# Two graph layers on one core: layer 1's weights turned through DRAM and VectorE, block results grown in place, v's bias joined to the output's, a new order of steps

## The chip, the cores and the metric

The kernel runs on one core of a Trainium2 chip. The metric is device time in microseconds of a whole launch, all loads and stores included. All data is float32.

## What is computed

128 batches of 128 nodes with 512 features pass through two layers, both with the same 128 x 128 adjacency. Layer 0 is attention with 8 heads; layer 1 weighs a node's neighbours by a leaky sum of two scores and puts an elu behind.

```python
def layer0(x):                       # Wq, Wk, Wv, Wo: 512 x 512
    q, k, v = x @ Wq + bq, x @ Wk + bk, x @ Wv + bv      # in 8 heads of 64
    s = q @ k.T / 8 + (1 - adj) * -1e9
    return (softmax(s) @ v) @ Wo + bo
def layer1(x):                       # W: 512 x 512, a = (a1, a2)
    h = x @ W
    e = leaky_relu((h @ a1)[:, :, None] + (h @ a2)[:, None, :], 0.2) * adj
    return elu(softmax(e) @ h + beta * h)
x = layernorm(x + layer0(x))
x = layernorm(x + layer1(x))
```

Layer 1 is computed in another order than written: the weights plus beta on the diagonal, A = softmax(e) + beta I, are applied to x first, and (A x) W is then one product.

## The kernel before, in words

Two batches make a group; there are 64 groups (`NG`). For each group five products with 512 x 512 weights are needed: q, k, v, the output product w and layer 1's h. Each is done by a scheme of seven half-size products in place of eight: the weights and the two batches are cut in 2 x 2 blocks, sums of blocks are made ahead (`weight_sum` once, `block_sum` on GpSimd per group), and the products 1, 2, 6, 7, 5, 3, 4 (`product`, lines 267 to 299) are added to each other into the four blocks of the result. Tiles named p (pq, pk, pv, pw, ph) and e (eq, ev, ew, eh) are their banks in PSUM. A q or k product is four matmuls of 128 columns, a v, w or h product two of 256; in the trace each fp32 matmul is two records.

Results leave PSUM in two ways. `take_part` (products 1, 6, 5) copies a product to a part buffer in SBUF, on ScalarE (for w on VectorE, which adds the residual). `take_block` (product 3) puts one straight into its block, and `add_block` (products 2, 7, 4) adds a product to a part and writes the block, on VectorE.

The other steps of a group, in the order of the data:

- `fetch_blocks`, `turn_x`: x is loaded in blocks and turned on VectorE (32 x 32 blocks, so the load does the outer part of the turn).
- `scores` (psc, line 381): 16 matmuls in a group, each on 64 of the 128 rows of the array. `mask`, `row_max`, `exps`, `row_inv`, `normalise` make the softmax on VectorE and ScalarE.
- `attn_write`, `attn_read`, `turn_attn`: the attention weights go to DRAM and come back with their 32 x 32 blocks in place, and VectorE turns the blocks.
- `attend` (po, line 456): 16 matmuls, each on 64 of the 128 columns. `attend_evict` (line 466) copies po to oT on VectorE and adds v's bias, which holds for each row because the softmax's rows sum to one.
- product w, with x + bo (`residual`, on GpSimd) added as it leaves; `bn_stats` and `norm_c` for the layer norm; `row_product` for layer 1's two scores.
- `spread_s2` (pb, line 535): two transposes on TensorE that spread the second score over all rows. `edge`, `leaky`, `edge_max`, `edge_exp`, `edge_inv`, `weights` make A in the tile att.
- `turn_weights` (pat, line 578): two transposes of A on TensorE; `weights_evict` (line 581) copies them to attT on ScalarE.
- `aggregate` (pz, line 591), `aggregate_evict`, product h, then elu, the second layer norm and `store`.

Nothing is scheduled at run time. `rows(g)` and `last_rows(g)` list each step with a place in us, relative to the group's start at g x `STEP` (line 19). For some groups, the first and the last, `other` gives a different list of places. `lay` collects them all, and the pieces are emitted sorted by place under `manual_schedule`: this sorted list is the order of the instructions on each engine, and each engine does its own in that order. The places come from a planner's costs and due times, and are not times of the chip. Groups overlap: a group's steps span about 170 us of places, so that while one is in its q and k products, the one before is in its w product and the one before that in its h product. All products draw on eight PSUM banks (`ps_mm`). DMAs of x, blocks, attention weights and stores are all issued from SP's queue, in the order of the list.

```python
    for g in range(NG):
        lay(g)
    ...
    with tc.manual_schedule():
        for _, _, fn, args in sorted(pieces, key=lambda p: p[:2]):
            fn(*args)
```

Of the kernel before, what the change touches and what calls it, by code (L numbers as in the profile page):

```python
# [13 lines left out]
P = 128  # L14
# [4 lines left out]
STEP = 37.33  # L19
# [3 lines left out]
def gnn_two_layers(  # L23
# [197 lines left out]
    xT, right, tx, qT, kT, vb, y, hp, main, side, part, oT, zT, xr = ({} for _ in range(14))  # L221
# [79 lines left out]
    def take(name, g, n, dst, half):  # L301

        src = region(name, g, n)
        if name in "vh":
            nc.scalar.copy(dst, src)  # L305
        else:
            for m in range(2):
                col = BIAS[name][:, 2 * half + m : 2 * half + m + 1]
                nc.scalar.activation(  # L309
                    dst[:, m, :], src[:, m * N : (m + 1) * N], AF.Identity, bias=col  # L310
                )

    def take_part(name, g, n, i, j):

        shape = [P, 2, N] if name in "qk" else [P, HF]
        t = wk2.tile(shape, F32, tag=f"part{name}{n}", name=f"part_{name}{n}_{g}", bufs=1)
        if name == "w":
            res = xr[g * G + j][:, i * HF : (i + 1) * HF]
            nc.vector.tensor_tensor(t, region(name, g, n), res, ALU.add)  # L319
        else:  # L320
            take(name, g, n, t, i)
        part[name, g, n] = t

# [31 lines left out]
    def take_block(name, g, i, j):  # L355
        dst = block(name, g, i, j)
        if name == "w":
            res = xr[g * G + j][:, i * HF : (i + 1) * HF]
            nc.vector.tensor_tensor(dst, region(name, g, 3), res, ALU.add)
        else:  # L360
            take(name, g, 3, dst, i)

    def add_block(name, g, i, j, n, m):
        src = region(name, g, n)
        if name in "qk":
            src = src.rearrange("p (m n) -> p m n", m=2)
        nc.vector.tensor_tensor(block(name, g, i, j), src, part.pop((name, g, m)), ALU.add)
# [95 lines left out]
    def attend_evict(b):  # L463

        oT[b] = wk2.tile([P, NC, N], F32, tag="oT", name=f"oT_{b}")
        nc.vector.tensor_tensor(  # L466
            oT[b], po.pop(b),
            later["bv"].rearrange("p (m o) -> p m o", o=1).broadcast_to([P, NC, N]), ALU.add,
        )
# [66 lines left out]

    def pair_rows(d, g, tag):
        if g not in d:
            d[g] = wk2.tile([P, G, N], F32, tag=tag, name=f"{tag}_{g}", bufs=1)
        return d[g]  # L540
# [27 lines left out]
    def weights(g, i):  # L568
        nc.vector.scalar_tensor_tensor(
            pair_rows(att, g, "att")[:, i, :], ee[g][:, i, :], einv[g][:, i : i + 1], beta_i,  # L570
            ALU.mult, ALU.add,
        )
# [66 lines left out]
    def at(place, fn, *args):  # L639
        pieces.append((place, len(pieces), fn, args))  # L640

    def rows(g):
# [3 lines left out]
            (-34.63, fetch_blocks, g), (-26.63, turn_x, g, 0), (-25.97, turn_x, g, 1),  # L646
            (-22.82, block_sum, "x", g, 1), (-22.08, block_sum, "x", g, 2),
            (-20.60, block_sum, "x", g, 3), (-19.86, block_sum, "x", g, 4),
            (-18.00, product, "q", g, 1), (-15.88, take_part, "q", g, 1, 0, 0),
            (-13.62, product, "k", g, 1), (-12.73, product, "q", g, 2),  # L650
            (-12.51, take_part, "k", g, 1, 0, 0), (-11.83, product, "k", g, 2),
            (-10.94, product, "q", g, 6), (-10.04, product, "k", g, 6),
            (-9.82, take_part, "q", g, 6, 1, 0), (-9.42, add_block, "k", g, 0, 0, 2, 1),
            (-9.15, product, "q", g, 7), (-8.93, take_part, "k", g, 6, 1, 0),
            (-8.00, product, "k", g, 7), (-7.11, product, "q", g, 5), (-6.81, fetch_x, b0),
            (-6.21, product, "k", g, 5), (-6.00, take_part, "q", g, 5, 1, 1),
            (-5.61, add_block, "q", g, 0, 0, 2, 1), (-5.53, fetch_x, b1),
            (-5.12, add_block, "q", g, 1, 1, 7, 5), (-5.10, take_part, "k", g, 5, 1, 1),
            (-4.45, product, "q", g, 3), (-4.22, add_block, "k", g, 1, 1, 7, 5),
            (-3.55, product, "k", g, 3), (-3.34, take_block, "q", g, 0, 1),  # L660
            (-2.44, take_block, "k", g, 0, 1), (-1.79, product, "q", g, 4),
            (-0.89, product, "k", g, 4), (0.10, add_block, "q", g, 1, 0, 4, 6),
            (0.19, residual, b0), (0.52, add_block, "k", g, 1, 0, 4, 6), (1.47, residual, b1),
            (1.97, scores, b0), (3.09, scores, b1), (3.31, mask, b0, 0), (3.98, mask, b0, 1),
            (4.44, product, "v", g, 1), (4.65, row_max, b0), (5.31, product, "v", g, 2),
            (5.53, take_part, "v", g, 1, 0, 0), (5.87, mask, b1, 0), (6.09, exps, b0, 0),
            (6.54, mask, b1, 1), (7.21, row_max, b1), (7.91, exps, b0, 1), (8.70, exps, b0, 2),
            (9.49, exps, b0, 3), (9.53, add_block, "v", g, 0, 0, 2, 1), (10.50, row_inv, b0),
            (10.92, normalise, b0, 0), (11.50, product, "v", g, 6), (11.52, normalise, b0, 1),
            (12.37, product, "v", g, 7), (12.59, take_part, "v", g, 6, 1, 0),  # L670
            (12.97, normalise, b0, 2), (13.57, normalise, b0, 3), (14.17, exps, b1, 0),
            (14.39, attn_write, b0), (14.96, exps, b1, 1), (16.45, exps, b1, 2),
            (16.72, product, "v", g, 5), (17.24, exps, b1, 3), (17.39, attn_read, b0),
            (18.03, take_part, "v", g, 5, 1, 1), (18.25, row_inv, b1), (18.67, normalise, b1, 0),
            (19.27, normalise, b1, 1), (19.52, add_block, "v", g, 1, 1, 7, 5),
            (20.25, normalise, b1, 2), (20.85, normalise, b1, 3), (21.67, attn_write, b1),
            (24.67, attn_read, b1), (25.56, turn_attn, b0, 0), (28.33, turn_attn, b0, 1),
            (31.06, turn_attn, b1, 0), (32.01, product, "v", g, 3),
            (33.10, take_block, "v", g, 0, 1), (33.53, turn_attn, b1, 1),
            (34.67, product, "v", g, 4), (35.76, add_block, "v", g, 1, 0, 4, 6),  # L680
            (37.33, attend, b0), (38.43, attend, b1), (38.65, attend_evict, b0),
            (45.35, product, "w", g, 1), (45.76, attend_evict, b1), (46.22, product, "w", g, 2),
            (46.44, take_part, "w", g, 1, 0, 0), (46.66, block_sum, "w", g, 3),
            (47.31, add_block, "w", g, 0, 0, 2, 1), (47.40, block_sum, "w", g, 1),
            (48.14, block_sum, "w", g, 2), (50.57, product, "w", g, 6),
            (51.44, product, "w", g, 7), (51.66, take_part, "w", g, 6, 1, 0),
            (53.32, block_sum, "w", g, 4), (54.92, product, "w", g, 5),
            (56.01, take_part, "w", g, 5, 1, 1), (56.43, add_block, "w", g, 1, 1, 7, 5),
            (57.55, product, "w", g, 3), (58.42, product, "w", g, 4),
            (58.64, take_block, "w", g, 0, 1), (59.06, bn_stats, y, b1, "c"),  # L690
            (59.75, bn_aggr, b1, "c"), (59.95, add_block, "w", g, 1, 0, 4, 6),
            (60.37, bn_stats, y, b0, "c"), (61.06, bn_aggr, b0, "c"), (61.26, add_eps, g, "c"),
            (61.43, row_product, b0, 0), (62.16, row_product, b0, 1), (62.89, inv_std, g, "c"),
            (63.61, row_product, b1, 0), (64.34, row_product, b1, 1), (65.07, scale_s, g),
            (66.32, norm_c, b0), (66.41, spread_s2, g), (66.88, edge, g, 0), (67.20, edge, g, 1),
            (67.53, leaky, g), (67.95, edge_max, g), (71.52, norm_c, b1), (72.88, edge_exp, g),
            (74.26, edge_inv, g), (74.43, weights, g, 0), (77.41, weights, g, 1),
            (78.65, turn_weights, g), (79.32, weights_evict, g), (80.84, aggregate, b0),
            (81.76, aggregate, b1), (81.98, aggregate_evict, b0), (84.42, product, "h", g, 1),
            (84.94, aggregate_evict, b1), (85.29, product, "h", g, 2),  # L700
            (86.21, block_sum, "h", g, 1), (86.78, take_part, "h", g, 1, 0, 0),
            (86.95, block_sum, "h", g, 2), (87.38, add_block, "h", g, 0, 0, 2, 1),
            (87.69, block_sum, "h", g, 4), (88.43, block_sum, "h", g, 3),
# [291 lines left out]
```

## Time and profile before

| | |
|---|---|
| time before, median of 3 runs | 2417.62 us (2417.3 to 2419.12) |
| the profiled execution's own time | 2414.03 us |
| its span, first to last instruction | 2412.2 us |
| TensorE busy in the span, matmuls / weight loads | 2387.4 / 2205.3 us |
| VectorE, ScalarE, GpSimd busy | 1957.7, 1485.5, 860.8 us |
| DMA | 245.30 MB, mean 102 GB/s |
| mean granted TensorE clock | 0.998 |

The views use short names: PE is TensorE's matmuls, PEld its weight loads, DVE VectorE, ACT ScalarE, POOL GpSimd, SP the engine whose queue issues most DMAs. Times are us unless marked ns. L289 is line 289 of the kernel. "pq<-xT,wq_sb" reads: writes tile pq from tiles xT and wq_sb; "128*64" is the part of TensorE's array that is used, rows by columns. In a timeline a row is a run of equal instructions with its start, its length and how many they are; matmuls overlap, so the length of a row reaches past the start of the next. In a table of groups, "x128 | 87.7, 686 | 16.5 <-PE po" says: 128 instructions, 87.7 us busy, 686 ns each, 16.5 us of idle time of the engine ahead of them, most of it ended by TensorE's po.

### The profile page before, as it was taken

How to read it: one execution, taken by the hardware profiler on the slowest of the kernel's cores; microseconds unless marked ns; L12 is line 12 of the kernel's file. 1: busy time of each engine (PE TensorE's matmuls, PEld its weight loads, DVE VectorE, ACT ScalarE, POOL GpSimd, SP SyncE). 2: the span in 40 equal slices, each digit the busy share in tenths (PEclk: the TensorE clock that was granted, in tenths of full speed). 3: DMA queues.
4: the chain of work that ended last, by engine and by line, in shares of the span. 5: the costliest groups of instructions: out<-in, count | busy, mean ns of one | idle time of the engine just before them, and what ended most of it. 6: DMA issues, size and time to landing. Idle time of an engine off the chain costs nothing.

```text
span 2412.2 us, 50040 instructions
## 1 busy us (share of the span) xinstructions
PE 2387.4 (99%) x17956; PEld 2205.3 (91%) x17956; DVE 1957.7 (81%) x4385; ACT 1485.5 (62%) x5310; POOL 860.8 (36%) x1045
## 2 busy tenths in 40 slices
PE   8999999999999999999999999999999999999998
PEld 8899999999999999999999999999999999999986
DVE  7788888888888887888888888888888787888887
ACT  4665665666656656666566566665665666656655
POOL 6332332333324323333243233332342333334322
PEclk9999999999999999999999999999999999999999
DMA  5323424334234243343342432433424324234332
GB/s 181 106 91 94 118 77 114 103 82 123 85 101 122 72 115 110 79 120 93 93 123 71 114 107 78 123 90 95 122 76 111 107 78 123 92 93 123 84 109 70
DMA packets 201336, 245.30 MB, mean 102 GB/s; under 512 B 18736, under 2 KB 149808, under 8 KB 200704
## 3 DMA queue, kind: packets, MB, share of 16 engines
q1 hardware_dynamic: 200144, 240.98, 34.7%
q8 instruction: 142, 2.33, 0.4%
q0 software_dynamic: 400, 0.86, 0.1%
q14 instruction: 106, 0.87, 0.1%
q10 hardware_dynamic: 544, 0.26, 0.0%
HBM read 141.37 MB, written 100.66 MB: 100 GB/s over the span
## 4 chain that ended last, share of the span: by engine, by line
PE 92%; DVE 3%; DMA 2%; ACT 1%; SPq 1%; issue 1%; POOL 0%; ACTq 0%; DVEq 0%; POOLq 0%
PE pw L289 11%; PE ph L289 11%; PE pq L295 11%; PE pv L289 11%; PE pk L295 11%; PE eq L295 9%; PE psc L381 5%; PE po L456 5%; PE pz L591 5%; PE ev L289 4%; PE eh L289 4%; PE ew L289 4%; PE pat L578 1%; DMA wv_sb<-in_L_gnn_Wv_dram 1%; ACT sb L417 1%
## 5 line engine op out<-in xcount | busy, mean ns | idle before, releaser
L403 ACT ACTIVATE s<-s,nmax 128x128 f32<-128x128 f32 x1024 | 397.7, 394 | 5.0 <-DVE nmax L397 5.0
L417 ACT ACTIVATE sb<-s,rinv 128x128 f32<-128x128 f32 x1024 | 327.1, 392 | 33.9 <-DVE rinv L410 22.9
L248 POOL TENSOR_TENSOR tw<-oT 128x256 f32<-128x256 f32 x63 | 45.7, 726 | 741.8 <-DVE oT L466 741.8
L437 POOL TENSOR_TENSOR x<-x,bo_b_in 128x512 f32<-128x512 f32 x128 | 164.0, 1291 | 381.0 <-DMA x<-in_x_dram 380.2
L309 ACT ACTIVATE part_q<-pq,bq_c 128x128 f32<-128x128 f32 x384 | 118.7, 360 | 236.9 <-PE pq L295 236.9
L403 ACT ACTIVATION_READ_ACCUMULATOR s<-s,nmax 128x1 f32 x1024 | 196.7, 192 | 0.0
L309 ACT ACTIVATE part_k<-pk,bk_c 128x128 f32<-128x128 f32 x384 | 119.9, 363 | 114.5 <-PE pk L295 67.0
L581 ACT COPY attT<-pat 128x256 f32<-128x256 f32 (+1 forms) x65 | 24.0, 368 | 266.5 <-PE pat L578 266.5
L389 DVE SCALAR_TENSOR_TENSOR s<-psc,amask 128x512 f32<-128x512 f32 x256 | 164.6, 683 | 25.1 <-PE psc L381 25.1
L446 DVE STREAM_TRANSPOSE attnT<-ab 128x512 f32<-128x512 f32 x256 | 178.8, 701 | 4.6 <-DMA ab<-scr 4.1
L506 DVE SCALAR_TENSOR_TENSOR ya<-w,wa_row 128x512 f32<-128x512 f32 x256 | 175.9, 687 | 4.4
L397 DVE TENSOR_REDUCE nmax<-s 128x8 f32<-128x1024 f32 x128 | 156.2, 1220 | 4.4
L319 DVE TENSOR_TENSOR part_w<-pw,x 128x256 f32<-128x256 f32 x189 | 79.4, 420 | 83.5 <-PE pw L289 83.1
L295 PE MATMUL pk<-xT,wk_sb 128*128 128x128 f32 x1024 | 139.9, 280 | 0.0
L228 DVE STREAM_TRANSPOSE xT<-xblk 128x512 f32<-128x512 f32 x128 | 134.7, 1096 | 5.1 <-DMA xblk<-in_x_dram 5.1
L295 PE MATMUL pq<-xT,wq_sb 128*128 128x128 f32 x1024 | 134.9, 275 | 0.8 <-DMA wq_sb<-in_L_gnn_Wq_dram 0.8
L295 PEld LDWEIGHTS pq<-xT,wq_sb 128*128 128x128 f32 x1024 | 129.4, 192 | 4.2 <-issue 1.0
L295 PEld LDWEIGHTS pk<-xT,wk_sb 128*128 128x128 f32 x1024 | 129.3, 192 | 3.9
L381 PE MATMUL psc<-kT,qT 64*128 64x128 f32 x2048 | 132.4, 279 | 0.0
L305 ACT COPY part_v<-pv 128x256 f32<-128x256 f32 x192 | 69.8, 364 | 99.3 <-PE pv L289 99.3
L381 PEld LDWEIGHTS psc<-kT,qT 64*128 64x128 f32 x2048 | 119.5, 188 | 12.1 <-issue 11.8
L591 PEld LDWEIGHTS pz<-attT,x 128*128 128x128 f32 x1024 | 124.3, 192 | 4.1 <-ACT attT L581 0.6
(676 smaller groups left out, 6588.2 us busy)
## 6 DMA issues: line engine op xcount, KB each, us to landing
scr<-sb SPq DMA_DIRECT2D x128, 512.0 KB, 2.7
ab<-scr SPq DMA_DIRECT2D x512, 128.0 KB, 3.1
x<-in_x_dram SPq DMA_DIRECT2D x128, 256.0 KB, 5.0
out_dram<-u SPq DMA_DIRECT2D x128, 256.0 KB, 2.1
xblk<-in_x_dram SPq DMA_DIRECT2D x254, 128.0 KB, 5.5
wq_sb<-in_L_gnn_Wq_dram SPq DMA_DIRECT2D x1, 1024.0 KB, 8.2
wk_sb<-in_L_gnn_Wk_dram SPq DMA_DIRECT2D x1, 1024.0 KB, 10.4
wv_sb<-in_L_gnn_Wv_dram SPq DMA_DIRECT2D x1, 1024.0 KB, 12.7
```

What stands on the lines that cost most here:

```text
L289: nc.tensor.matmul(out, b[:, c, :], a[:, c, :], start=first and c == 0, stop=(c == 1), skip_group_check=True,)
L295: nc.tensor.matmul(out[:, m * N : (m + 1) * N], a[:, c, m * P : (m + 1) * P], b[:, c, :], start=first and m == 0 and c == 0, stop=(c == 1) ...
L309: nc.scalar.activation(dst[:, m, :], src[:, m * N : (m + 1) * N], AF.Identity, bias=col)
L381: nc.tensor.matmul(psc[b][j][:, m, :], qT[g][feats, m, rows], kT[g][feats, m, rows], start=True, stop=True,)
L389: nc.vector.scalar_tensor_tensor(s_t[b][:, j * HP : (j + 1) * HP, :], psc[b][j], SCALE, amask.rearrange("p (o n) -> p o n", o=1).broadcast ...
L397: nc.vector.tensor_reduce(nmax[b], s_t[b], AX.X, ALU.max, negate=True)
L403: nc.scalar.activation(s_t[b][:, h, :], s_t[b][:, h, :], AF.Exp, bias=nmax[b][:, h : h + 1], accum_out=rsum[b][:, h : h + 1],)
L417: nc.scalar.mul(sb[b][:, :, h, :], s_t[b][:, h, :].rearrange("p (b c) -> p b c", c=Q), rinv[b][:, h : h + 1],)
L437: nc.gpsimd.tensor_tensor(xr[b], xr[b], later["bo"], ALU.add)
L446: nc.vector.transpose(attnT[b].rearrange("p h (a r) -> p a h r", r=Q)[:, rows], ab[b].rearrange("p a (h c) -> p a h c", c=Q)[:, rows],)
L506: nc.vector.scalar_tensor_tensor(z, y[b], 1.0, wa_row[j], ALU.mult, ALU.mult, accum_out=s12[g][:, i, j : j + 1])
L591: nc.tensor.matmul(pz[b][:, c, :], x1[b][:, c * P : (c + 1) * P], attT[g][:, i, :], start=True, stop=True,)
```

## The change

- In groups 0 to 61 (`by_blocks`) layer 1's weights are no longer turned on TensorE. `weights` writes att with its 32-column blocks outermost; `weights_write` sends it to DRAM (128 KB, 1 KB a row), four `weights_read` bring it back with blocks in place (32 KB each, runs of 256 bytes), and `weights_turn` turns the 32 x 32 blocks on VectorE into attT. The last two groups keep `turn_weights`.
- `attend_evict` becomes a plain copy on ScalarE. v's bias is carried through the output product once: `bias_product` makes bv @ Wo on TensorE, `bias_add` adds it to bo.
- Part buffers go. `take_part` (now products 1, 6, 5 and 3) writes the block itself, and `add_block` adds a product to the block in place. The engines of these steps stay as they were.
- `STEP` goes from 37.33 to 36.928, and the lists of places are all new: `rows`, `last_rows` (which now has a list for each of the last two groups), `other`, and the places of the weights' loads and sums. In the steady order the two batches' scores have v's and w's first products between them; `attend` comes for the second batch first; w1's load comes after wo's.

```diff
-STEP = 37.33
+STEP = 36.928
...
-    def take_part(name, g, n, i, j):
-
-        shape = [P, 2, N] if name in "qk" else [P, HF]
-        t = wk2.tile(shape, F32, tag=f"part{name}{n}", name=f"part_{name}{n}_{g}", bufs=1)
...
+    def take_part(name, g, n, i, j):
+
+
+        src, dst = region(name, g, n), block(name, g, i, j)
+        if name in "vh":
+            nc.scalar.copy(dst, src)
+        elif name == "w":
             res = xr[g * G + j][:, i * HF : (i + 1) * HF]
-            nc.vector.tensor_tensor(dst, region(name, g, 3), res, ALU.add)
+            nc.vector.tensor_tensor(dst, src, res, ALU.add)
...
-        nc.vector.tensor_tensor(block(name, g, i, j), src, part.pop((name, g, m)), ALU.add)
+        nc.vector.tensor_tensor(dst, src, dst, ALU.add)
...
     def attend_evict(b):
-
         oT[b] = wk2.tile([P, NC, N], F32, tag="oT", name=f"oT_{b}")
-        nc.vector.tensor_tensor(
-            oT[b], po.pop(b),
-            later["bv"].rearrange("p (m o) -> p m o", o=1).broadcast_to([P, NC, N]), ALU.add,
-        )
+        nc.scalar.copy(oT[b], po.pop(b))
+
+
+    bop = {}
+
+    def bias_product():
+        bop[0] = ps_mm.tile([P, D], F32, tag="mm", name="bop")
+        for c in range(NC):
+            nc.tensor.matmul(
+                bop[0], later["bv"][:, c : c + 1].broadcast_to([P, P]), wo_sb[:, c, :],
+                start=(c == 0), stop=(c == NC - 1),
+            )
+
+    def bias_add():
+        nc.vector.tensor_tensor(later["bo"], bop[0], later["bo"], ALU.add)
...
+    def by_blocks(g):
+
+        return g < NG - 2
+
+    def weights_write(g):
+        att_d[g] = scr.tile([P, 4, G * Q], F32, tag="attd", name=f"attd_{g}")
+        nc.sync.dma_start(
+            out=att_d[g].rearrange("p b e -> p (b e)"), in_=att[g].rearrange("p i n -> p (i n)")
+        )
+
+    def weights_read(g):
+        ab2[g] = wk2.tile([P, 4, G * Q], F32, tag="ab2", name=f"ab2_{g}", bufs=1)
+        for n in range(4):
+            nc.sync.dma_start(
+                out=ab2[g][n * Q : (n + 1) * Q],
+                in_=att_d[g][:, n, :].rearrange("(a r) e -> r a e", r=Q),
+            )
+
+    def weights_turn(g):
+        nc.vector.transpose(
+            pair_rows(attT, g, "attT").rearrange("p i (a r) -> p a i r", r=Q),
+            ab2[g].rearrange("p a (i c) -> p a i c", c=Q),
+        )
...
-            (1.97, scores, b0), (3.09, scores, b1), (3.31, mask, b0, 0), (3.98, mask, b0, 1),
-            (4.44, product, "v", g, 1), (4.65, row_max, b0), (5.31, product, "v", g, 2),
...
+            (1.047, scores, b0), (2.042, product, "v", g, 1), (2.317, mask, b0, 0),
+            (2.472, mask, b0, 1), (3.328, scores, b1), (4.811, row_max, b0),
+            (5.124, product, "v", g, 2), (5.419, take_part, "v", g, 1, 0, 0),
...
+            (34.656, add_block, "v", g, 4, 1, 0), (35.86, attend, b1), (36.604, attend, b0),
+            (39.077, attend_evict, b1), (39.294, attend_evict, b0), (39.343, product, "w", g, 1),
...
+            (73.77, weights, g, 1), (75.158, weights_write, g), (75.942, weights_read, g),
+            (81.449, weights_turn, g), (84.036, aggregate, b0), (85.026, aggregate, b1),
...
-        own = last_rows(g) if g == NG - 1 else rows(g)
+        own = rows(g) if g < NG - 2 else last_rows(g)
...
-    at(15.205, load_weight, w1_sb, w1)
-    at(15.265, load_later)
...
-    at(21.105, load_weight, wo_sb, wo)
...
+    at(-2.505, load_later)
...
+    at(13.895, load_weight, wo_sb, wo)
...
+    at(16.595, load_weight, w1_sb, w1)
...
+    at(26.176, bias_product)
...
+    at(29.816, bias_add)
```

## The prediction

> **What bounds the kernel now.** I read the page first, then the chain of waits over some laps, then TensorE's timeline. The page:
>
> ```profile
> span 2412.2 us, 50040 instructions
> PE 2387.4 (99%) x17956; PEld 2205.3 (91%) x17956; DVE 1957.7 (81%) x4385; ACT 1485.5 (62%) x5310; POOL 860.8 (36%) x1045
> PE   8999999999999999999999999999999999999998
> ```
>
> TensorE has work in every slice, and no other engine is near it. The chain of waits, in order of time, repeats itself once per group of two batches:
>
> ```profile
> 714.28 1.90 PE po L456 x32
> 739.40 0.98 PE pk L295 x8
> 751.26 1.90 PE po L456 x32
> ```
>
> One lap is 751.26 - 714.28 = 36.98 us, wholly TensorE. A product that TensorE no longer does is saved, and whatever slows its stream is paid. So I take the stream apart. In TensorE's timeline a step's price is the start of the next row less its own start:
>
> ```profile
> 712.33 1.05 PE L295 MATMUL eq<-tx,wq_sb 128*128 128x128 f32 x8
> 713.22 1.06 PE L295 MATMUL eq<-tx,wk_sb 128*128 128x128 f32 x8
> 714.21 1.97 PE L456 MATMUL po<-attnT,v 128*64 128x128 f32 x32
> 716.11 2.06 PE L381 MATMUL psc<-kT,qT 64*128 64x128 f32 x32
> 718.09 0.44 PE L578 MATMUL pat<-ident,att 128*128 128x128 f32 x2
> 718.37 1.89 PE L289 MATMUL pv<-wv_sb,xT 128*128 128x256 f32 x8
> ```
>
> A q or k product takes 0.89 us, but 0.99 when po follows, which works in half-width tiles (128*64). Both batches' scores (psc, 64*128) together take 1.98, the two transposes of the weights (pat) 0.28, of which only 0.22 is work: the like pair pb takes 0.21 elsewhere (742.90 to 743.11). Near the end the score runs of the two batches stand apart:
>
> ```profile
> 2350.50 1.16 PE L381 MATMUL psc<-kT,qT 64*128 64x128 f32 x16
> 2351.59 1.13 PE L289 MATMUL pw<-wo_sb,oT 128*128 128x256 f32 x4
> 2352.65 1.16 PE L381 MATMUL psc<-kT,qT 64*128 64x128 f32 x16
> 2353.74 1.13 PE L289 MATMUL pv<-wv_sb,xT 128*128 128x256 f32 x4
> 2354.71 1.03 PE L289 MATMUL pw<-s_w,tw 128*128 128x256 f32 x4
> 2355.57 0.60 PE L289 MATMUL pv<-s_v,tx 128*128 128x256 f32 x2
> ```
>
> Each run takes 1.09, the product between them 1.06 and the one after 0.97, where an undisturbed one takes 0.86. Every change of tile shape costs.
>
> **The Trainium skill.** "TensorEngine Tiling (Array Packing)", Key Properties, says that changing the tiling mode, not just the tile, drains TensorE. The trace agrees: about 0.1 us on each side of a change. It gives no figure; I use the trace's. "DMA: Bandwidth & Descriptors", Anatomy of one DMA, puts a fixed cost of about 2 us on a DMA, most of it the receipt; here 256 KB stores land in 2.1 us, 512 KB writes in 2.7, reads in 3.1. Its section on small descriptors charges 27% for 256-byte ones, the size of the new reads; no such transfer is in this trace. "VectorE: DVE Perf Modes", The three transpose paths: VectorE turns 32x32 blocks only, which is why the new path needs the DRAM trip.
>
> **The change, part by part.** Counts are from the order of the two built kernels.
>
> *Transposes off TensorE:* 128 fall to 4; 62 groups x 0.22 us = **-13.6 us**, all on the path.
>
> *v's bias:* four 512-column products once. The like plw rows take 1.71 us for two (2374.60 to 2376.31): **+3.4 us**; between 0, if they fill a wait of the start, and 3.4; I take all. The added addition (0.69 us, once) is VectorE's.
>
> *The new order:* a lap now runs po, po, scores of the first batch, v's and w's first products, scores of the second, v, w. The order changes from score tiles back to full ones 124 times instead of 66, and from full ones to score tiles 63 times instead of 6: 57 laps have the split. Its price: two runs apart 2.18 against 1.98 together, +0.20; the two products between lose 0.20 (1.06 against 0.86); the one after 0.11; the 0.06 that pat paid goes. 0.45 x 57 = **+25.7 us**. The other split in the trace (from 2312.41) shows the same 1.09 twice. Ends: 0.40 and 0.50, so 23 to 28.
>
> *A wait that goes:* the pk row of the chain takes 0.98 instead of 0.89. Its weight load waits for ScalarE to evict k's first product, one product earlier. In the new order two products of h (1.73 us) stand between: 57 x 0.09 = **-5.1 us**. It could come back elsewhere: 0 to -5.1.
>
> *oT's eviction* moves to ScalarE:
>
> ```profile
> L466 DVE TENSOR_TENSOR oT<-po,bv_c 128x512 f32<-128x512 f32 x128 | 87.7, 686 | 16.5 <-PE po L456 16.4
> L446 DVE STREAM_TRANSPOSE attnT<-ab 128x512 f32<-128x512 f32 x256 | 178.8, 701 | 4.6 <-DMA ab<-scr 4.1 <-issue 0.4
> L598 ACT COPY zT<-pz 128x512 f32<-128x512 f32 x128 | 73.0, 570 | 4.2 <-PE pz L591 4.2
> ```
>
> VectorE loses 2 x 0.686 us a lap and gains one transpose of 256 columns, between 0.35 (half of attnT's) and 0.55 (half of xT's 1.096): about 1 us a lap less. ScalarE gains 2 x 0.57 and loses weights_evict's 0.372: 23.2 of 37 us become 24. Neither bounds, so 0. Cover: after po the second copy ends some 0.8 us later, while w's first product stands behind a score run and v's product (2.06 us): 1.2 us of margin.
>
> *Weights through DRAM.* In the new order 16.1 us of TensorE work stand between pb and the aggregation (five q/k/v products 4.5, po 1.9, scores 2.2, eight products with their switches 7.3, pb 0.2). The chain needs: two edges 0.69, leaky 0.54, max 0.42, exponentials 1.18, reciprocal 0.16, weights 0.70, the write 2.1 to 2.7, four reads (three issues of 0.47 apart, then 3.1) 4.5, the transpose 0.35 to 0.55, ten handovers of about 0.1: 12 to 13 us. Margin 3 us: 0. If VectorE reaches the transpose late, behind it wait the reciprocal and the second half of the masks, and for those ScalarE's exponentials; TensorE waits in pz. On SP's queue the write stands behind the four block loads and ahead of the next scores' write, which isn't due for 8 us; five more issues of 0.43 us a lap fit SP's idle time. Block loads move ahead of the point where they were late in some laps.
>
> *In place:* the same number of evictions and additions; the first write of a block now waits for the last reader of the group before, several us earlier in every case: 0. ScalarE's waits on part buffers (47 us) were idle time off the path.
>
> *Start, stray laps, end.* At the start v's first product no longer stands where it waited 2.5 us for wv, with slow products after: -4. But w1's load is moved behind a block load and wo on SP (all those bytes had landed at 29.1 us, w1 at 24.1), and VectorE's wa_column and TensorE's wa_turn wait for it: +1.5. From 122.6 to 2273.4 us, 58 laps take 6.0 us more than 58 x 36.98, mostly products waiting for late additions and restarting slowly:
>
> ```profile
> PE pq L295 <- DVE qT L367: 3.5, 8, 1.3
> PE eq L295 <- DVE kT L367: 2.9, 2, 1.7
> ```
>
> VectorE's lighter lap should recover a third: -2. The last groups' order is new, with as many products: 0, give or take 2.
>
> **Sum:** -13.6 + 3.4 + 25.7 - 5.1 - 2.5 - 2 = **+5.9 us**. On the profiled execution (span 2412.2, its time 2414.0) that gives 2419.9; the median, 2417.6, lies 3.6 above that execution, and with it the forecast is **2423.5 us**.
>
> **Rivals.** *More waits recovered:* TensorE's products and changes alone come to 2371 us before; start, end and waits are the other 41. If the new orders save 10 instead of 4.5 of these, 2418. For it: 12 us are lost before 123 us. Against: the start still waits for loads. *A new wait in every lap:* ScalarE's exponentials end the longest waits of VectorE (rinv, 94.8 us in 62 waits), and behind rinv of the second batch stand some 6.4 us of VectorE work before the addition to h on which a product waits; I work out about 1 us of margin. At 0.3 us a lap over 60 laps, 2441. *Faster:* the split costs little, because the weight loads of the next shape are taken ahead. At 0.35 us a lap the change is neutral (19.8/57), below 0.26 it is faster by over 0.2%; at 0.1 it gives 2403. Against it stand two splits in the trace.
>
> **Chances** (0.2%, 4.8 us, is about what a measurement here can tell from no change). Forecast 0.55, by itself 2418 to 2430: slower 0.31, same 0.24. More recovered 0.20: same 0.17, faster 0.03. New wait 0.17: slower. Cheap split 0.08: faster. Slower 0.48, same 0.41, faster 0.11. The range runs from 2413, within the second case, to 2438, the lower half of the third.
>
> **What would show it.** Right: a lap near 37.1 us; two score rows of 1.09 with a dearer product between; no pat rows but four; pk at 0.89; no wait in pz for attT. Wrong: a score row of about 1.0 with undisturbed neighbours; a wait of TensorE that recurs in each lap, by attT or h; over 8 us saved before 120 us.

## The result, and the profile after

| | before | after |
|---|---|---|
| median of 4 runs each, on one chip | 2417.46 us | 2486.09 us (2485.13 to 2488.85) |
| ratio, 95% interval | 1 | 1.0287 (1.0269 to 1.0305): slower |
| span of the profiled execution | 2412.2 us | 2483.3 us |

The forecast was 2423.5 us with a range from 2413 to 2438: right in its sign, and 62.6 us short. The forecast was 5.9 us more than before; measured are 68.6 us more. The page of after, span and busy time of the engines:

```profile
span 2483.3 us, 50325 instructions
PE 2415.6 (97%) x17840; PEld 2187.2 (88%) x17840; DVE 1954.7 (79%) x4320; ACT 1528.5 (62%) x5376; POOL 839.3 (34%) x1045
```

TensorE's share falls from 99% to 97%, though nothing else is near it: it now waits somewhere, and a share of the whole span can't say where. The chain of waits of after, in order of time, over the same stretch as before:

```profile
734.84 1.90 PE po L442 x32
...
757.64 0.91 PE pk L295 x8
758.55 0.02 issue
758.57 0.63 ACT kT L343 x2
759.20 0.70 ACT u L644
759.90 0.27 ACT h L337
760.17 0.04 issue
760.22 1.13 PE ph L289 x4
...
773.06 1.90 PE po L442 x32
```

One lap is 773.06 - 734.84 = 38.22 us, against 36.98 before and about 37.1 forecast; and it is no longer wholly TensorE. In its middle the chain leaves TensorE for 1.7 us: from k's second product to ScalarE, through the eviction of k's **first** product, a layer norm (L644) and the copy of h's product 6, and only then back to h's product 5. TensorE's timeline of the same moment, and ScalarE's:

```profile
757.48 1.05 PE L295 MATMUL pk<-xT,wk_sb 128*128 128x128 f32 x8
758.37 1.06 PE L295 MATMUL pq<-tx,s_q 128*128 128x128 f32 x8
760.22 1.13 PE L289 MATMUL ph<-w_sb,th 128*128 128x256 f32 x4 [0.79 <-ACT h L337]
761.18 1.05 PE L295 MATMUL eq<-tx,s_q 128*128 128x128 f32 x8
```

```profile
758.57 0.63 ACT L343 ACTIVATE kT<-pk,bk_c 128x128 f32<-128x128 f32 x2 [1.75 <-PE pk L295]
759.09 0.81 ACT L644 ACTIVATE u<-u,nmr,rstdf_('f',16)_7622 128x512 f32<-128x512 f32 x1
759.79 0.37 ACT L337 COPY h<-ph 128x256 f32<-128x256 f32 x1
```

The q product from 758.37 should take 0.89; the next start (760.22) comes 1.85 later, 0.96 too late, and h's product 5 itself then takes 0.96 instead of 0.86: it restarts slowly. Together 1.06 us. ScalarE, 62% busy, stood idle for 1.75 us just before, waiting for TensorE. The table of waits (total us, number of waits, longest) says that this is in nearly every lap:

```profile
PEld ph L289 <- ACT h L337: 58.6, 61, 1.5
PE ph L289 <- ACT h L337: 46.4, 59, 1.3
```

59 x 1.05 = 62 us, which is what the forecast lacks. Around the score runs, TensorE's timeline shows what was forecast:

```profile
736.66 1.16 PE L367 MATMUL psc<-kT,qT 64*128 64x128 f32 x16
737.75 1.13 PE L289 MATMUL pv<-wv_sb,xT 128*128 128x256 f32 x4
738.72 1.03 PE L289 MATMUL pw<-wo_sb,oT 128*128 128x256 f32 x4
739.68 1.16 PE L367 MATMUL psc<-kT,qT 64*128 64x128 f32 x16
740.77 1.13 PE L289 MATMUL pv<-wv_sb,xT 128*128 128x256 f32 x4
741.74 1.03 PE L289 MATMUL pw<-wo_sb,oT 128*128 128x256 f32 x4
```

Two runs of 1.09, two products between them at 1.93 (1.73 undisturbed), 0.97 for the one behind.

**Why ScalarE waits for the second product.** k's products 1 and 2 are the two halves of one PSUM bank. In before the list had the eviction of product 1 ahead of product 2, so product 2 waited for ScalarE (the 0.98 of the pk row in the prediction). TensorE's row and ScalarE's in before:

```profile
739.24 1.14 PE L295 MATMUL pk<-xT,wk_sb 128*128 128x128 f32 x8
```

```profile
738.54 0.62 ACT L309 ACTIVATE part_k<-pk,bk_c 128x128 f32<-128x128 f32 x2 [0.67 <-PE pk L295]
```

In after the list has product 2 first (places -16.248 and -15.957), and the eviction waits for product 2's end. Some such order has to be kept: the Trainium skill, "PSUM — Partial Sum Buffer", PSUM bank collisions raise a hardware error, says that TensorE's write and ScalarE's read must not meet in one bank and quadrant, whichever columns they touch, and asks for guards by bank, not by address. The traces fit a wait by bank: in after ScalarE is held until 758.57 by a product whose half it doesn't read. What happens without the wait no run here shows. So **the wait was turned round**: it left TensorE's queue and went into ScalarE's. The same page's section Engine vs sequencer instructions calls ScalarE's queue strict FIFO, and the trace agrees: the norm and the copy stand behind and run only when the eviction is through (from 759.09 and 759.79).

That is theory A. Rivals: B, growth in place makes the copy of h's product 6 wait for VectorE's addition into the same tile; C, the split score runs cost far more than 0.45 us.

### The profile page after: what moved, and what is told of

The parts are those of the page before. It is cut to its first block, busy times and chain, and to the rows that moved or that the text cites. A ratio compares the mean times of both kernels' runs of the same rounds, so it can differ in the third digit from the quotient of the medians.

```text
span 2483.3 us, 50325 instructions
## 1 busy us (share of the span) xinstructions
PE 2415.6 (97%) x17840; PEld 2187.2 (88%) x17840; DVE 1954.7 (79%) x4320; ACT 1528.5 (62%) x5376; POOL 839.3 (34%) x1045
## 4 chain that ended last, share of the span: by engine, by line
PE 91%; ACT 5%; DMA 2%; DVE 1%; issue 0%; SPq 0%; DVEq 0%; ACTq 0%
PE pv L289 12%; PE ph L289 11%; PE pk L295 11%; PE pw L289 11%; PE pq L295 9%; PE eq L295 9%; PE psc L367 5%; PE po L442 5%; PE pz L614 5%; PE ev L289 4%; PE ew L289 4%; PE eh L289 4%; ACT u L644 2%; ACT kT L343 1%; ACT h L337 1%; DMA wv_sb<-in_L_gnn_Wv_dram 1%
## 5 line engine op out<-in xcount | busy, mean ns | idle before, releaser
L343 ACT ACTIVATE kT<-pk,bk_c 128x128 f32<-128x128 f32 x512 | 160.2, 364 | 289.4 <-PE pk L295 155.0
L403 ACT ACTIVATE sb<-s,rinv 128x128 f32<-128x128 f32 x1024 | 314.7, 399 | 3.0 <-DVE rinv L396 1.8
L337 ACT COPY v<-pv 128x256 f32<-128x256 f32 x256 | 94.6, 370 | 301.1 <-PE pv L289 301.0
L502 DVE SCALAR_TENSOR_TENSOR ya<-w,wa_row 128x512 f32<-128x512 f32 x256 | 205.0, 801 | 4.4
L343 ACT ACTIVATE qT<-pq,bq_c 128x128 f32<-128x128 f32 x512 | 160.9, 367 | 49.4 <-PE pq L295 49.2
L337 ACT COPY h<-ph 128x256 f32<-128x256 f32 x252 | 93.6, 371 | 151.5 <-PE ph L289 151.5
L248 POOL TENSOR_TENSOR tw<-oT,oT 128x256 f32<-128x256 f32 x63 | 45.8, 727 | 357.2 <-ACT oT L451 346.9
L353 DVE TENSOR_TENSOR h<-eh,h 128x256 f32<-128x256 f32 x126 | 53.4, 424 | 126.2 <-ACT h L337 98.0
L367 PE MATMUL psc<-kT,qT 64*128 64x128 f32 x2048 | 148.3, 285 | 0.0
L289 PE MATMUL pv<-wv_sb,xT 128*128 128x256 f32 x512 | 144.3, 404 | 0.0
```

Of the source, the lines that this page charges most:

```text
L289: nc.tensor.matmul(out, b[:, c, :], a[:, c, :], start=first and c == 0, stop=(c == 1), skip_group_check=True,)
L343: nc.scalar.activation(dst[:, m, :], src[:, m * N : (m + 1) * N], AF.Identity, bias=BIAS[name][:, 2 * i + m : 2 * i + m + 1],)
L367: nc.tensor.matmul(psc[b][j][:, m, :], qT[g][feats, m, rows], kT[g][feats, m, rows], start=True, stop=True,)
L403: nc.scalar.mul(sb[b][:, :, h, :], s_t[b][:, h, :].rearrange("p (b c) -> p b c", c=Q), rinv[b][:, h : h + 1],)
L502: nc.vector.scalar_tensor_tensor(z, y[b], 1.0, wa_row[j], ALU.mult, ALU.mult, accum_out=s12[g][:, i, j : j + 1])
```

## The experiments

The medians of before were 2412.85 us beside the first four kernels, 2413.33 beside the next four and 2419.58 beside the last three; so ratios to these are compared, and times only within one set. A change of a place holds for the steady list, that is for most groups; the diffs of places leave out the lines between.

### h's copy ahead of k's eviction

```diff
 in the steady list of places
-  (95.313, take_part, "h", g, 6, 1, 0)
+  (94.816, take_part, "h", g, 6, 1, 0)      # ahead of take_part k 1
```

> After, with one 0.26 us copy moved on ScalarE's queue: the eviction of h's product 6 stands ahead of that of k's product 1. Theory A (the wait turned round): k's first eviction now waits for k's second product, ScalarE idles 1.75 us there, the copy of h's product 6 stands behind it and one norm, and h's product 5 waits 0.95 us and restarts slowly. Then the stall goes whole: 59 x 1.05 = 62 us less, lap 37.15, about 2424. Theory B (in place: the copy waits for VectorE's addition into the same tile): it waits wherever it stands, no change, about 2486. Theory C (the split score runs cost three times my 0.45 us): no change, about 2486.

2427.48 us, ratio 1.006 (1.0043 to 1.0077). The lap is 37.17 us. ScalarE's timeline, then TensorE's:

```profile
742.42 0.37 ACT L337 COPY h<-ph 128x256 f32<-128x256 f32 x1
744.17 0.62 ACT L343 ACTIVATE kT<-pk,bk_c 128x128 f32<-128x128 f32 x2 [1.38 <-PE pk L295]
```

```profile
743.97 1.06 PE L295 MATMUL pq<-tx,s_q 128*128 128x128 f32 x8
744.86 1.03 PE L289 MATMUL ph<-w_sb,th 128*128 128x256 f32 x4
```

One copy of 0.26 us, moved ahead of k's eviction and one norm, takes the stall away: the lap falls by 1.05 us. ScalarE still idles 1.38 us for the second product; now that costs nothing that TensorE's timeline shows, since the copy is no longer behind it. A holds; B and C expected no change.

### k's eviction ahead of k's product 2

```diff
-  (-15.957, take_part, "k", g, 1, 0, 0)
+  (-16.26, take_part, "k", g, 1, 0, 0)      # product k 2 is at -16.248
```

> After, with the eviction of k's product 1 issued ahead of k's product 2, as it was before. Theory A: ScalarE no longer waits for product 2; it evicts at about 756.8 to 757.4 of the lap that I looked at, so h's product 5 waits no more, but k's product 2, due at 757.4, waits up to 0.3 us and restarts: 59 x (1.05 less 0 to 0.4), lap 37.15 to 37.55, 2424 to 2448. Theories B and C: no change, about 2486.

2431.99 us, ratio 1.0078 (1.0063 to 1.0093), lap 37.17: the same lap from the other side. k's product 2 takes 0.90, so ScalarE is in time and the feared 0.3 us don't come. The 4.5 us above the last kernel are mostly one early lap of 43.91 us in place of 39.34, with one wait of 3.3 us of pk for kT.

### Growth in place undone

```diff
+        if n != 3:
+            dst = part[name, g, n] = wk2.tile(shape, F32, tag=f"part{name}{n}", ..., bufs=1)
...
-        nc.vector.tensor_tensor(dst, src, dst, ALU.add)
+        old = part.pop((name, g, {2: 1, 7: 5, 4: 6}[n]))
+        nc.vector.tensor_tensor(dst, src, old, ALU.add)
```

> After, with growth in place undone alone: products 1, 6, 5 go to part tiles of their own and the additions read these, as before. Theory A: the wait for k's second product is PSUM's, nothing changes, 2486 give or take 4. Theory B: the copy of h's product 6 no longer waits for VectorE, the stall goes, about 2424.

2486.73 us, ratio 1.0304 (1.0288 to 1.0319); after's 1.0287 lies in that interval. h's product 5 still waits 46.3 us in 59 waits for the copy, now to a part tile; and this kernel takes 59 us more than the one with the copy ahead, measured in the same set. B falls: growth in place doesn't make the stall. The lap is 38.17 us against 38.21 in most laps of after; these 0.04 come up again below.

### The score runs together

```diff
-  (2.042, product, "v", g, 1)
-  (39.343, product, "w", g, 1)
+  (3.345, product, "v", g, 1)               # scores of b1 are at 3.328
+  (40.28, product, "w", g, 1)
```

> After, with the first products of v and w behind both score runs instead of between them. Prediction's price of the split, 0.45 x 57 = 26 us: about 2460, and the stall of h's product 5 stays. Theory C: over 60 us less, about 2424 or below. A cheap split (0.1 us a lap): 2480.

2463.64 us, ratio 1.021 (1.0195 to 1.0226): 23 us below the kernel with the part tiles, in the same set (lap 37.82), and the stall of h's product 5 is still there (47.2 us in 59 waits). C falls.

### Both edits: faster than either kernel

> After with both edits: h's product 6 evicted ahead of k's product 1, and the score runs together. If the two costs are independent, the sum of what each alone gave: 2427.5 less 22.5 (2486.1 to 2463.6), lap about 36.8 us, about 2405, which is under both kernels. If one hid part of the other: 2412 to 2425.

2403.47 us, ratio **0.9958** (0.9944 to 0.9972). The two costs add up. The score runs and the lap (two neighbouring rows of TensorE's timeline of this kind):

```profile
715.28 2.06 PE L367 MATMUL psc<-kT,qT 64*128 64x128 f32 x32
...
752.05 2.06 PE L367 MATMUL psc<-kT,qT 64*128 64x128 f32 x32
```

36.77 us, 0.21 under before: once the two costs of the order are out, the change as a whole saves.

### The weights back on TensorE

The first kernel of these experiments, with `turn_weights` and `weights_evict` in the places of the write, the reads and the turn, in every group.

> The kernel with h's product 6 ahead (2427.5), with the weights turned on TensorE in every group, and ScalarE to evict them. The prediction's price: 60 x 0.22 = 13.2 us more, about 2441, lap 37.38. If the DRAM path cost hidden time elsewhere, less than 8 more.

2440.76 us, ratio 1.0114 (1.0099 to 1.0129), against 1.006 (measured in another set): 13 us by the ratios, give or take some 5, and 13.2 were forecast. The lap says more: 37.34 us, 0.17 above 37.17 and not 0.22. In TensorE's timeline pat takes its 0.22, but a product of w (pw from s_w) takes 0.86 here and 0.91 with the weights through DRAM, so that in this order the transposes' removal brings about 10 us net and not 13.6.

### Before, with only the scores split

First both of v's products between the score runs, then only the first:

```diff
-  (4.44, product, "v", g, 1), (5.31, product, "v", g, 2)
+  (2.4, product, "v", g, 1), (2.5, product, "v", g, 2)      # both between
+  (2.4, product, "v", g, 1), (5.31, product, "v", g, 2)     # one between
```

> Before, with v's first two products between the two batches' score runs, nothing else. The prediction's price without the term for the product that follows (0.40 a lap, pat follows the second run as it did): 58 x 0.40 = 23 us more, about 2437, lap 37.38. By what undoing it gave in after (22.5 us): the same. If the split itself is cheap and the order around it was the cost in after: under 8 us more.

2482.53 us, ratio 1.0284 (1.0269 to 1.03): 69 us more, not 23. TensorE's timeline shows what I had overlooked (the next row starts at 742.17):

```profile
738.30 1.16 PE L381 MATMUL psc<-kT,qT 64*128 64x128 f32 x16
739.39 0.44 PE L578 MATMUL pat<-ident,att 128*128 128x128 f32 x2
740.29 2.05 PE L591 MATMUL pz<-attT,x 128*128 128x128 f32 x16 [0.46 <-ACT attT L581]
```

v's products had stood between pat and pz and had covered the eviction of pat. Without them pat to pz takes 0.90 us instead of 0.28, and pz restarts slowly (1.88 instead of 1.78): 0.72 of the lap's 1.12 us are that, and 0.40 the split. So the kernel was a poor test, and the second one puts the cover back:

> Before, with v's first product alone between the two batches' score runs; v's second stays between the transposes of the weights and the aggregation, and covers their eviction (0.37 us and the way there), which the kernel with both products between did not do. The price of the split by the prediction's rows: 0.20 for the runs and 0.20 for the product: 58 x 0.40 = 23 us more, about 2437, lap 37.38, no wait in pz. If the last kernel's 69 us were the split's own: about 2482.

2441.48 us, ratio 1.0096 (1.0076 to 1.0116): 22 us more. TensorE's timeline:

```profile
722.33 1.16 PE L381 MATMUL psc<-kT,qT 64*128 64x128 f32 x16
723.42 1.13 PE L289 MATMUL pv<-wv_sb,xT 128*128 128x256 f32 x4
724.48 1.16 PE L381 MATMUL psc<-kT,qT 64*128 64x128 f32 x16
725.58 0.44 PE L578 MATMUL pat<-ident,att 128*128 128x128 f32 x2
725.85 1.03 PE L289 MATMUL pv<-wv_sb,xT 128*128 128x256 f32 x4
726.72 1.95 PE L591 MATMUL pz<-attT,x 128*128 128x128 f32 x16
```

From the first score run to pz it is 4.39 us, 3.99 before: 0.40 a lap.

### Before, with only the wait turned round

```diff
-  (-11.83, product, "k", g, 2)
+  (-12.52, product, "k", g, 2)              # ahead of take_part k 1, at -12.51
```

> Before, with k's product 2 issued ahead of the eviction of product 1, so that ScalarE waits for the product and no longer TensorE for ScalarE; the order on each engine is unchanged. If the turned wait costs only by what stands behind it on ScalarE (there, in before, only q's sixth product, whose own end comes later): the 0.09 us a lap go and nothing comes, 58 x 0.09 = 5 us less, about 2408. If a turned wait costs by itself: 0.3 us a lap or more, over 2430.

2415.67 us, ratio 1.001 (1.0003 to 1.0016): no loss, but no gain either. ScalarE's wait for pk goes from 67.0 us to 173.3, in the table of waits, and TensorE's timeline shows where the 0.09 us went (the next row starts at 705.64):

```profile
702.87 1.06 PE L295 MATMUL pk<-xT,wk_sb 128*128 128x128 f32 x8
703.77 1.06 PE L295 MATMUL pq<-tx,s_q 128*128 128x128 f32 x8
704.66 1.15 PE L295 MATMUL pk<-tx,s_k 128*128 128x128 f32 x8
```

k's second product is back at 0.90, and k's product 6 takes 0.98. It overwrites what the late eviction reads, which runs from 703.97 to 704.59, close ahead of it; that this is its wait is read from these times and not tried. So the 5 us forecast for this kernel don't come, but neither does the loss of over 0.3 us a lap: a turned wait is not dear by itself, its price is what stands behind it.

### One layer norm behind the copy

```diff
-  (131.956, norm_f, b1)
+  (132.284, norm_f, b1)                     # behind take_part h 6 in ScalarE's queue
```

> After, with one layer norm (0.70 us of ScalarE's queue) moved from ahead of the eviction of h's product 6 to behind it, in 55 laps; the eviction of k's product 1 stays ahead. If h's product 5 starts when k's second product has ended and everything queued ahead of its eviction is through, the stall shrinks by just that norm: 55 x 0.70 = 38 us less, about 2448, and 0.25 to 0.35 us a lap stay. If the norm isn't on that path: no change, 2486. If the norm alone makes the stall: 2427.

2448.38 us, ratio 1.0125 (1.0108 to 1.0142), lap 37.51 us: after less 0.71, the length of the norm. What is left of the stall, in TensorE's timeline:

```profile
750.47 1.06 PE L295 MATMUL pq<-tx,s_q 128*128 128x128 f32 x8
751.61 1.13 PE L289 MATMUL ph<-w_sb,th 128*128 128x256 f32 x4
752.57 1.05 PE L295 MATMUL eq<-tx,s_q 128*128 128x128 f32 x8
```

0.25 us of waiting and 0.10 of slow restart, together the upper end of what was forecast to stay. So the stall is a plain sum, by the chain of after: eviction 0.63, norm 0.70, copy 0.27 and handovers 0.06 from the end of k's second product make 1.66 us, of which q's product covers the 0.71 until 759.26.

### oT's eviction back on VectorE

The fastest kernel, with `attend_evict` as in before and no bias product.

> The kernel with both edits (2403.5), with v's bias and oT's eviction back on VectorE and no bias product. The prediction costs the eviction's move at nothing and the product at 3.4: about 2400. If VectorE's load matters (1.37 us a lap more): 0.1 us a lap or more, 2406 and up.

2430.44 us, ratio 1.005 (1.0035 to 1.0065), against 0.9958 in another set: 22 us more, though the bias product is gone. The lap is 37.19 us against 36.77, that is 24 us in 58 laps. Table of waits and chain of waits of this kernel:

```profile
PEld pw L289 <- DVE w L340: 31.6, 60, 0.7
```

```profile
724.44 0.57 DVE oT L451
725.02 0.60 DVE s L375
725.61 0.60 DVE oT L451
726.21 0.61 DVE s L375
726.82 0.02 issue
726.84 1.22 DVE nmax L383
728.06 0.34 DVE w L340
728.41 0.04 issue
728.45 1.13 PE pw L289 x4
```

w's products now come right behind the scores, and w's second one waits for VectorE's eviction of the first, which stands behind 3.6 us of both oT, two masks and a maximum. In this order, with the score runs together, the move to ScalarE is no side issue: it is worth 0.42 us a lap. In after's own order it was not tried.

## Why the prediction was wrong, by its own steps

**The step that failed** is "A wait that goes": it counted 57 x 0.09 us as saved, said that "it could come back elsewhere: 0 to -5.1", so that at worst the saving would be nothing, and a loss was left out. It asked what stands between product 2 and its wait on TensorE's queue. It didn't ask which wait comes in place of the one removed, on which queue, and what is queued behind it there. By the places in the new list the eviction of product 1 comes after product 2, so ScalarE must wait for a product that starts 2.6 us later, and behind it stand 0.70 us of norm and the copy that h's product 5 needs. Shown by four runs: the copy moved ahead and the eviction moved ahead (each takes the stall whole), the norm moved (0.71 of 1.05 us), and growth in place undone (the stall stays).

In the 58 laps from group 3 to group 61 (first score run of 122.57 to 2273.41 before, 123.29 to 2341.88 after) the difference is 67.8 us. Forecast were 58 x 0.14 less 2 = 6.1; the turned wait adds 58 x 1.05 = 61. The kernel with the copy ahead, free of the stall, has a lap of 37.17 us, close to the 37.1 forecast, and is slower than before by 0.6%, so the sign was no luck. The rest of the step came true: k's second product takes 0.89 again. The head of the run differs by 0.7 us (forecast 0.9: the bias product's 3.4 less the start's 2.5) and the end by 2.6 (forecast 0, give or take 2); no run takes these apart.

**The rivals.** "A new wait in every lap" was the right kind, and "a wait of TensorE that recurs in each lap, by attT or h" was its sign. But it was put on VectorE's queue, with an addition to h, at 0.3 us; it came on ScalarE's, with a copy, at 1.05.

**The terms that held.**

- Transposes off TensorE, -13.6: putting them back cost 13 by the ratios, 0.17 us a lap by the trace, since the product of w named below got faster with it.
- The split, +25.7: 0.40 us a lap where it is joined again (37.17 to 36.77) or made in before. The prediction's 0.45 had 0.05 more because pat's 0.06 gave way to 0.11 of a product, which a joined run pays too.
- The bias product, +3.4: its eight records start from 33.8 to 36.8 us, 0.43 us apart. That is the size forecast; whether they fill a wait of the start wasn't tried by itself.
- Weights through DRAM at nothing: the write landed in 1.7 us, the reads in 1.8 each and the turn took 0.434 us; in after pz waits for attT only in the last two groups, where TensorE still turns (1.4 us in 2 waits). The prediction's list of this chain adds up to 11.6 to 12.4 us, not 12 to 13; nothing hangs on it.
- In place at nothing: undoing it changed the lap by 0.04 us, and the stall not at all.
- Stray laps, -2: the 58 laps of before take 6.0 us more than 58 x 36.98, those of after 2.4 more than 58 x 38.21. The reason given, a lighter VectorE, is not what happened: oT's 87.7 us left it and the turn's 26.9 came, but it was busy for 1954.7 us against 1957.7. Other steps got longer, ya (the sums for layer 1's scores) from 175.9 to 205.0 us. So this number came out by luck, as far as the runs show.

**oT's eviction at nothing** was right as a price of the move, as far as the runs show: after's table of waits has no wait of TensorE for the copy. It missed that the order with the scores together needs the move: left on VectorE, oT's eviction costs 24 us in 58 laps there.

Not settled: the 0.05 us by which one w product (pw from s_w, product 6) takes 0.91 in after and 0.86 in before, 3 us in all. It takes 0.86 or 0.87 in three kernels made from after: with growth in place undone, with the weights back on TensorE, and with oT on VectorE. In after its weight load idles 0.19 us and starts at 744.27, just behind VectorE's addition of w's product 2, which reads the same bank from 743.77 to 744.16. This fits one more wait by bank, now for VectorE; no run tries it by itself.

## What to carry to other kernels

When a change swaps a product and the eviction of its bank's other half, the wait need not vanish but can change queues, as it did here: look up what the newly waiting engine has queued behind, up to the next instruction that the bounding engine needs. An engine at 62% can still end each lap's longest wait. And when a step is moved, ask what its old place was covering: v's products covered pat's eviction, and one copy of 0.26 us moved ahead in its queue was worth some 60 us here.

## What the runs showed that I had not expected

- A product that has waited for another engine is itself slower once: 0.96 instead of 0.86 us for h's product 5, 1.88 instead of 1.78 for pz. Each of these two stalls cost about 0.1 us a lap on top of its gap.
- Small runs did not hold the new DMAs up: four reads of 32 KB in runs of 256 bytes landed in 1.8 us each. The 128 KB reads in runs of 1 KB took 3.0, but as the sizes differ too, this doesn't say what a small run costs. The fixed cost of about 2 us that the prediction takes from the Trainium skill, "DMA: Bandwidth & Descriptors", Anatomy of one DMA, is stated there for DMAs that GpSimd issues; these are issued from SP, and the whole write of 128 KB landed in 1.7 us.
- ScalarE waits as well for VectorE's read of another half of a bank: 134.0 us in 61 waits of kT for the addition into kT in after, and 135.8 in 61 with growth in place undone, so it isn't the tile in SBUF. In before it was 47.4 in 59; the prediction took these for waits on part buffers, but they grew when the part buffers went. The Trainium skill, "PSUM — Partial Sum Buffer", PSUM bank collisions raise a hardware error, counts reads against reads too. In the chain of after's lap no step comes from these waits.
